# Linear attention in 32x32 tiles over four pairs, with turns in blocks of 32 on VectorE

## The chip, the cores and the metric

The kernel runs on one core of a Trainium2 chip. The metric is the time of one execution on the device in microseconds (us), from the first to the last instruction of the core; lower is better. A profile is one such execution, taken by the hardware profiler. Engines are called PE (TensorE), PEld (its weight loads), DVE (VectorE), ACT (ScalarE), POOL (GpSimd) and SP (the engine that issues the DMAs).

## The reference

The input x has 16 images of 256 channels and 64 x 64 pixels, in fp32. There are two layers, each with a group normalization ahead of it and the input added behind it. The first is a grouped 3x3 convolution whose weights are rotated per image, times a factor per channel. The second is linear attention with 8 heads of 32 channels, and a depthwise 5x5 sum of the values:

```
q, k, v = xt @ Wq.T + bq, ...           # xt: tokens x channels of the normalized image
q = (relu(q) + 1e-06) / scale           # k likewise
q = q**3 / norm(q**3) * norm(q)         # k likewise
z = 1 / (q . k.sum(tokens) + 1e-06)     # per token and head
out = (q @ (k.T @ v)) * z + depthwise5x5(v)
out = out @ Wproj.T + bproj
```

## The kernel before

Images are worked through one after the other; parts of image b + 1 (its convolution) and of image b + 2 (statistics of its input) are put between the steps of image b. The order is written out by hand: each engine does its instructions in the order of the source, so that an instruction that waits holds up all behind it on its engine. All DMAs are issued by SP, in order too. The tokens of an image are taken in 32 tiles of 128; two of them make a pair m, and an image has NP = 16 pairs.

*Key steps* (`key_step`, L718; 16 per image, of which the first three are done inside the attention of the image before). `key_products` multiplies two tiles by the key and value weights (L525, 128x512), `key_bias` adds the bias and applies relu on DVE, `squares` (ACT), `cube` (POOL, L504), `ratio` (DVE) and `root` (POOL, L513) make the factor norm / norm, `key_scale` (ACT) applies it, `values` (L558) sums k.T @ v and the keys' sum over the tokens in two PSUM banks. `key_store` writes the values to DRAM (vpad), from which `load_blocks` reads them back as vh for the depthwise sum.

*Between* (`between`, L741): the first query products, the first of the four convolutions of the next image (`convolve`, L358: 9 taps, each in 16 tiles of 32x32 at once, into four banks), the last values, the depthwise sum of the first half (`depthwise`, L593, 8 x 16 products into fm by ACT).

*Attention steps* (`attention_step`, L779; one per pair, with the steps of neighbouring pairs one behind the other). `blocked` (L610, ACT) copies a pair's pixels into blocks of 8 x 4, `query_products` (L618) and `query_bias` make q with the tokens on the partitions; `squares`, `cube`, `ratio`, `root` give its factor. `turn` (L634, PE) and `turned` (L639, ACT) put the channels on the partitions. `attend` (L642) multiplies by the masked state kvx (L651), so that the result has the tokens on the partitions and 33 columns per head, the last of which is the denominator: z has 16 numbers per partition (two tiles, 8 heads; L653, L656), the product with z (L660, DVE) and the sum with fm (L662, POOL) follow. `turn_back` (L670, PE; L672, ACT) turns it, `project` (L680) multiplies by Wproj, `add_up` (L692, DVE) adds bias and input, and `store` writes two pairs at a time. Convolutions 1 to 3 of the next image are begun in steps 3, 7 and 11 (UNITS) and moved out in the step behind (`evict`, L371, ACT; `settle`, L381 and L382, DVE); the rows for each are loaded into one buffer, xr, by `load_rows`. The second half of the depthwise sum is in step 9 (SECOND). fm, xr and vh have one buffer each. Five PSUM banks go round (`bank`), two hold the sums of values and then pn (kv0, kv1), one the small products.

`more_stats` (L700) takes the statistics of a part of image b + 2 on DVE (L107) and issues the load of the next part, which goes into the same buffer. `prepare` (L184) makes the rotated weights of image b + 2.

Of the kernel before, what the change touches and what calls it, by code (L numbers as in the profile page):

```python
# [9 lines left out]
F32 = mybir.dt.float32  # L10
# [5 lines left out]
P = 128  # L16
C = 256
# [11 lines left out]


UNITS, SECOND = {3: 1, 7: 2, 11: 3}, 9

STATS = {3: (0, 1), 5: (2,), 7: (3, 4), 9: (5, 6), 11: (7,)}
# [6 lines left out]
NV = 6  # L40
# [6 lines left out]
K_ID, K_G8, K_GM, K_CG, K_SG, K_SEL, K_END = 0, 128, 256, 260, 278, 296, 424  # L47
# [3 lines left out]
def conv_attention(ctx: ExitStack, tc: tile.TileContext, x, consts, kw, b1, w2, b2, b2r,  # L51
# [11 lines left out]
    rp = pool("rows", 2)  # L63
    op = pool("outs", 2)
# [4 lines left out]
    ps = pool("ps", 5, space=PSUM)  # L69
    psk = pool("psk", 1, space=PSUM)  # L70
    pss = pool("pss", 1, space=PSUM)
# [43 lines left out]
    ident = ct[:, K_ID:K_ID + P]  # L115
# [11 lines left out]
    phalf = const("phalf", [P, 2])  # L127
    nc.gpsimd.memset(phalf, 0.5)
    pi2 = const("pi2", [P, 1])
# [21 lines left out]
    def gn_coefs(st, b, which):  # L151
# [6 lines left out]
        mean, var = mv[:, :, 0], mv[:, :, 1]  # L158
        co = sp.tile([P, 5, 2], F32, tag=f"co{which}", name=f"co{which}_{b}")
        a, pooled, d, v, m = (co[:, k, :] for k in range(5))  # L160
        pm = pss.tile([P, 2], F32, tag="small", name=f"pm{which}_{b}")
# [6 lines left out]
        pv = pss.tile([P, 2], F32, tag="small", name=f"pv{which}_{b}")  # L168
# [5 lines left out]
        if which == 0:  # L174
            nc.vector.tensor_mul(pooled, d, a)
        return a, pooled, m
# [7 lines left out]
    def prepare(b):  # L184
# [9 lines left out]
        ph = pss.tile([HID, 2], F32, tag="small", name=f"ph_{b}")  # L194
# [8 lines left out]
        pa = pss.tile([P, 2 + 2 * HD], F32, tag="small", name=f"pa_{b}")  # L203
# [21 lines left out]
        pe = pss.tile([P, NH], F32, tag="small", name=f"pedge_{b}")  # L225
# [63 lines left out]
        def shifts(t):  # L289


            pb = pss.tile([P, 3], F32, tag="small", name=f"pbias_{b}_{t}")
# [6 lines left out]
            nc.vector.tensor_scalar(shift[:, t, 3:4], shift[:, t, 3:4], -1.0, None, ALU.mult)  # L299
# [66 lines left out]
    def evict(b, u, q):  # L366

        i, t = 2 * u + q // 2, q % 2
        if t == 0:
            state[b]["x"][i] = xp.tile([P, 2, CH], F32, tag="x", name=f"x_{b}_{i}")  # L370
        nc.scalar.activation(state[b]["x"][i][:, t, :], state[b]["pc"][q], AF.Identity,  # L371
                             bias=state[b]["shift"][:, t, 3:4])

    def settle(b, u, q):
# [5 lines left out]
        e = xt[:, t, :].rearrange("p (r w) -> p r w", w=W)[:, :, 0:W:W - 1]  # L380
        nc.vector.tensor_add(e, e, shift[:, t, 0:3:2].unsqueeze(1).to_broadcast([P, ROWS, 2]))  # L381
        nc.vector.bn_stats(state[b]["st1"][:, t, i, :], xt[:, t, :])  # L382

    load_kernels(0)
    for _ in prepare(0):
        pass
# [5 lines left out]
    wp_t = const("wp", [P, 2, C], halves(wp))  # L392
    bp_t = const("bp", [P, 2], bp)
    dwb_t = const("dwb", [P, 2], dwb)
# [34 lines left out]
    for (w, br), lo in zip(wl.values(), (0, 2 * C)):  # L429
        for t in range(2):  # L430
            nc.vector.tensor_mul(w[:, t, 0:C], w[:, t, 0:C], inv_t)
        nc.vector.tensor_mul(br[:, 0:C], br[:, 0:C], inv_t[0:1])
        n = w.shape[2]
        nc.sync.dma_start(wscr[:, :, lo:lo + n], w)
        nc.sync.dma_start(bscr[:, lo:lo + n], br)

    pb = pss.tile([P, 2], F32, tag="small", name="pb")
    for co in range(2):
        for t in range(2):
            nc.tensor.matmul(pb[:, co:co + 1], lhsT=wp_t[:, t, ts(co, P)], rhs=dwb_t[:, t:t + 1],  # L440
                             start=t == 0, stop=t == 1)
    nc.vector.tensor_add(bp_t, bp_t, pb)
# [47 lines left out]
    def focus(r, name):  # L490
        return {"r": r, "name": name, "s": sp.tile([P, 4, 2], F32, tag="s", name=f"s_{name}", bufs=5)}

    def relu(f):
        nc.vector.scalar_tensor_tensor(f["r"], f["r"], 0.0, eps_t.unsqueeze(1).to_broadcast([P, 2, C]),  # L494
                                       ALU.max, ALU.add)
# [10 lines left out]
    def ratio(f, inverse):  # L506
        s2, s6, q = (f["s"][:, k, :] for k in range(3))
        over, under = (s6, s2) if inverse else (s2, s6)
        nc.vector.reciprocal(q, under)
        nc.vector.tensor_mul(q, q, over)  # L510
# [479 lines left out]
```

## Time and profile before

| what | value |
| --- | --- |
| time, median of 3 runs | 3762.31 us (3759.23 to 3769.41) |
| the profiled execution: time / span | 3763.77 us / 3762.0 us |
| granted PE clock, mean | 0.988 |
| busy: PE / PEld / DVE / ACT / POOL | 95% / 74% / 65% / 54% / 44% |
| DMA | 513.78 MB, 137 GB/s, share of 16 engines 44.3% |

A row of the groups names line, engine, operation, what is written and read, shapes and count; behind the bar stand the busy time in us and the mean of one instruction in ns; behind the second bar the idle time of the engine ahead of it and what ended it. A row of the timeline has the start in us, the length of the merged piece, and the same names. A row of stages has the stretch, its length, the busy time of PE, PEld, DVE, ACT and POOL with their instructions, the granted clock, the share of the DMA engines and their GB/s. Ends of PE's instructions are modelled and reach into the next one; starts are exact. Each fp32 product is two records on PE, each fp32 turn one. DVE's idle time is no cost as long as another engine sets the end.

### The profile page before, as it was taken

Reading aid. Unit: us, or ns where it says so; the run is one execution under the profiler, and the core shown is the slowest. Engines: PE = TensorE matmul, PEld = TensorE weight load, DVE = VectorE, ACT = ScalarE, POOL = GpSimd, SP = SyncE. Lnnn points to the kernel's source line nnn. Section 1 sums busy time; section 2 is a strip of 40 time slices with the busy share of each in tenths; the row PEclk is TensorE's granted clock in tenths of the full one; section 3 lists DMA queues with packets and bytes.
Section 4 is the critical chain, followed back from the end, with each engine's and each line's share of the span. In section 5 each row is a group of like instructions: output and inputs, shape, how many; then the busy total and the mean of one; then the engine's idle time right before and its main releaser. Section 6 shows DMA issues by size and latency. Waiting matters only on the chain. (4 is left out here: it accounts for less than half of the span.)

```text
span 3762.0 us, 102026 instructions
## 1 busy us (share of the span) xinstructions
PE 3568.1 (95%) x40424; PEld 2769.5 (74%) x40424; DVE 2435.6 (65%) x6403; ACT 2013.1 (54%) x6501; POOL 1638.3 (44%) x1775
## 2 busy tenths in 40 slices
PE   5899999999999999999999999999999999999999
PEld 3577777777777777687777777777777777777778
DVE  5756667566675656667666675666856667566656
ACT  2455645556455555654646455464555645555555
POOL 3343535344353444534445353343534535344445
PEclk9999999999999999999999999999999999999999
DMA  6453544525445254452634535355353544524332
GB/s 175 130 155 95 156 145 128 171 83 159 144 143 164 81 169 126 145 169 87 175 114 148 169 100 175 94 153 156 110 175 95 155 145 145 163 77 151 103 131 105
DMA packets 219807, 513.78 MB, mean 137 GB/s; under 512 B 26645, under 2 KB 99863, under 8 KB 207044
## 3 DMA queue, kind: packets, MB, share of 16 engines
q1 hardware_dynamic: 219332, 507.26, 44.3%
q8 instruction: 320, 5.24, 0.6%
q14 instruction: 155, 1.27, 0.1%
HBM read 371.63 MB, written 135.53 MB: 135 GB/s over the span
## 5 line engine op out<-in xcount | busy, mean ns | idle before, releaser
L525 PE MATMUL pk<-wkv,x 128*128 128x512 f32 x2048 | 989.4, 624 | 0.0
L662 POOL TENSOR_TENSOR o<-o,fm 128x256 f32<-128x256 f32 x512 | 362.9, 730 | 1045.0 <-DVE o L660 890.1
L525 PEld LDWEIGHTS pk<-wkv,x 128*128 128x128 f32 x2048 | 611.4, 312 | 191.3 <-issue 16.1
L358 PE MATMUL pc<-xr,wt 32*32 32x504 f32 (+1 forms) x17856 | 616.9, 596 | 8.2 <-issue 4.2
L358 PEld LDWEIGHTS pc<-xr,wt 32*32 32x32 f32 x17856 | 360.7, 103 | 227.2 <-issue 88.3
L680 PE MATMUL py<-oT,wp 128*128 128x256 f32 x2048 | 507.2, 390 | 11.8 <-ACT oT L672 11.7
L618 PE MATMUL pq<-wq,xq 128*128 128x256 f32 x2048 | 492.0, 383 | 22.4 <-ACT qT L639 20.4
L501 ACT ACTIVATE r_k<-rk 128x256 f32<-128x256 f32 x1024 | 415.4, 407 | 177.2 <-DVE rk L494 109.7
L371 ACT ACTIVATE x<-pc,shift 128x512 f32<-128x512 f32 x256 | 165.4, 690 | 527.7 <-PE pc L358 527.7
L501 ACT ACTIVATE r_q<-rq 128x256 f32<-128x256 f32 x1024 | 413.9, 408 | 59.0 <-POOL rq L504 32.3
L618 PEld LDWEIGHTS pq<-wq,xq 128*128 128x128 f32 x2048 | 370.0, 191 | 84.8 <-ACT qT L639 27.1
L680 PEld LDWEIGHTS py<-oT,wp 128*128 128x128 f32 x2048 | 368.0, 189 | 60.5 <-ACT oT L672 15.8
L672 ACT COPY oT<-po 128x512 f32<-128x512 f32 x256 | 150.0, 586 | 455.4 <-PE po L670 454.9
L626 DVE TENSOR_TENSOR rq<-pq,bq 128x512 f32<-128x512 f32 x256 | 176.1, 688 | 335.5 <-PE pq L618 328.2
L513 POOL TENSOR_TENSOR s_k<-s_k,phalf 128x2 f32<-128x2 f32 x256 | 177.0, 692 | 483.8 <-DVE s_k L510 472.7
L547 ACT ACTIVATE rk<-rk,s_k 128x256 f32<-128x256 f32 x512 | 231.8, 500 | 243.5 <-POOL s_k L513 243.5
L533 DVE TENSOR_TENSOR rk<-pk,bkv 128x256 f32<-128x256 f32 x512 | 214.7, 419 | 225.5 <-PE pk L525 222.6
L504 POOL TENSOR_TENSOR rk<-r_k,rk 128x512 f32<-128x512 f32 x256 | 326.8, 1277 | 66.2 <-ACT r_k L501 65.4
L558 PEld LDWEIGHTS pkv<-v,rk 128*128 128x128 f32 x2048 | 271.1, 194 | 111.2 <-issue 51.8
L504 POOL TENSOR_TENSOR rq<-r_q,rq 128x512 f32<-128x512 f32 x256 | 329.7, 1288 | 29.9 <-issue 29.9
L513 POOL TENSOR_TENSOR s_q<-s_q,phalf 128x2 f32<-128x2 f32 x256 | 179.4, 701 | 368.2 <-DVE s_q L510 366.8
L558 PE MATMUL pkv<-v,rk 128*128 128x132 f32 x2048 | 275.1, 281 | 21.5 <-ACT rk L547 21.5
(128 smaller groups left out, 5369.9 us busy)
## 6 DMA issues: line engine op xcount, KB each, us to landing
vh<-vpad SPq DMA_DIRECT2D x256, 384.0 KB
vh<-vpad SPq DMA_DIRECT2D x256, 360.0 KB
vpad<-v SPq DMA_DIRECT2D x512, 128.0 KB
out<-x SPq DMA_DIRECT2D x128, 512.0 KB
xr<-in_x SPq DMA_DIRECT2D x186, 320.0 KB
xs<-in_x SPq DMA_DIRECT2D x224, 256.0 KB
xr<-in_x SPq DMA_DIRECT2D x62, 288.0 KB
xs<-in_x SPq DMA_DIRECT2D x16, 512.0 KB
```

The lines of the kernel that those rows point to most:

```text
L358: nc.tensor.matmul(pcs[q].rearrange("p (r w) -> p r w", w=W)[ts(j, HD), :, to:to + n], lhsT=wt[ts(q, HD), j, k, :], rhs=g[ts(q, HD), j, r: ...
L501: nc.scalar.activation(f["r2"][:, j, :], f["r"][:, j, :], AF.Square, accum_out=f["s"][:, k, j:j + 1])
L504: nc.gpsimd.tensor_mul(f["r"], f["r2"], f["r"])
L513: nc.gpsimd.tensor_tensor(f["s"][:, 3, :], f["s"][:, 2, :], phalf, ALU.pow)
L525: nc.tensor.matmul(pm, lhsT=state[b]["x"][n // 2][:, t, T % BC:CH:BC], rhs=w[:, t, :], start=t == 0, stop=t == 1)
L533: nc.vector.tensor_add(f["r"][:, j, :], pm[:, 0:C], br[:, 0:C])
L547: nc.scalar.mul(f["r"][:, j, :], f["r"][:, j, :], f["s"][:, 3, j:j + 1])
L558: nc.tensor.matmul(pkv[hh], lhsT=r[:, j, ts(hh, P)], rhs=vbuf[n % NV][:, j, :, 4 * hh:4 * hh + 4], start=T == 0, stop=T == NT - 1,)
L618: nc.tensor.matmul(pq[:, j, :], lhsT=xq[:, t, ts(j, P)], rhs=w[:, t, :], start=t == 0, stop=t == 1)
L626: nc.vector.tensor_add(f["r"], f["pq"], state[b]["q"][1].unsqueeze(1).to_broadcast([P, 2, C]))
L662: nc.gpsimd.tensor_add(o, o, fm[:, 2 * (m % NCH) + j, :])
L680: nc.tensor.matmul(py[:, co].rearrange("p y (J c) -> p J y c", c=BC), lhsT=wp_t[:, t, ts(co, P)], rhs=oT[:, t, :].rearrange("p (J y c) -> ...
```

## The change

Attention now goes over a group g of PG = 4 pairs at once, four groups per image, and keeps the channels on the partitions behind it.

- `evict` writes the convolved image in the order of blocks (8 x 4 pixels), so that `blocked` is gone and the queries read it directly; it adds the projection's bias as well (in shift). The two edge columns are corrected by POOL, once for both halves of the channels, instead of by DVE. The statistics take the bias out and put it back (`gn_coefs`).
- The queries are scaled on ACT (`scale`), and `ratio` and `root` are done for two pairs of queries at once. The 1e-06 of relu is in the bias; relu is one tensor_tensor with max.
- `query_turn`: DVE turns the queries in blocks of 32x32 (one instruction of 128x512 per pair, 16 per image) instead of PE and ACT.
- `spread_state`: one product spreads the state over four row groups; kvd holds, per half a and head d of four, a 32x32 block of the state (k = 0) and the keys' sum repeated over 32 columns (k = 1).
- `attend(b, g, a)`: 32 products of 32x32 tiles with 256 columns, 16 tiles at once, into four banks: per partition 256 numerators and 256 denominators, one per channel. There are 8 of them per image.
- `divide`: ACT copies the denominators out and adds 1e-06, DVE takes the reciprocal of 128x512 and multiplies it with the numerators, twice per half group. `join` adds it on POOL to fm in place.
- `depthwise` gives fm by head and channel; `turn_blocks` turns it in blocks on DVE, in place (two instructions of 128x1024 per group).
- `project` multiplies 512 columns at a time, straight from fm; `turn`, `turned` and `turn_back` are gone. `add_up` adds x and writes into fm, and the store goes out from there.
- Six banks go round, and all the small products and pn take theirs among them. The scratch tiles of rows (tag r1) have four buffers. The values have five buffers instead of six.
- The order of the steps is new (`between`, `group`, `lead`). Query pairs 0 to 3 are made in `between`; group g makes the queries of group g + 1. Convolutions 1, 2 and 3 stand in groups 0, 1 and at the head of group 2, the second half of the depthwise sum behind convolution 3, the three early key steps of the next image in group 3. The rows of the next convolution are loaded at the end of groups 0 and 1.
- The setup computes the projection's bias ahead of the first kernels.

The diff, cut (of functions that are rewritten, the new lines; the old ones stand above):

```diff
-    ps = pool("ps", 5, space=PSUM)
+    ps = pool("ps", 6, space=PSUM)
     psk = pool("psk", 1, space=PSUM)
-    pss = pool("pss", 1, space=PSUM)
...
-        nc.scalar.activation(state[b]["x"][i][:, t, :], state[b]["pc"][q], AF.Identity,
+        xt = state[b]["x"][i][:, t, :].rearrange("p (J y c) -> p y J c", y=BR, c=BC)
+        nc.scalar.activation(xt, state[b]["pc"][q].rearrange("p (y J c) -> p y J c", y=BR, c=BC), AF.Identity,
                              bias=state[b]["shift"][:, t, 3:4])
     def settle(b, u, q):
         if u == 0 and q == 0:
             state[b]["st1"] = sp.tile([P, 2, NCH, 6], F32, tag="st1", name=f"st1_{b}")
         xt, shift = state[b]["x"][i], state[b]["shift"]
-        e = xt[:, t, :].rearrange("p (r w) -> p r w", w=W)[:, :, 0:W:W - 1]
-        nc.vector.tensor_add(e, e, shift[:, t, 0:3:2].unsqueeze(1).to_broadcast([P, ROWS, 2]))
+        if t == 0:
+            e = xt[:, 0, 0:1]
+            e = bass.AP(e.tensor, e.offset, [e.ap[0], [CH, 2], [BC, BR], [CH - BR * BC + BC - 1, 2]])
+            nc.gpsimd.tensor_add(e, e, shift[:, :, 0:3:2].unsqueeze(2).to_broadcast([P, 2, BR, 2]))
...
-        nc.vector.scalar_tensor_tensor(f["r"], f["r"], 0.0, eps_t.unsqueeze(1).to_broadcast([P, 2, C]),
-                                       ALU.max, ALU.add)
+        nc.vector.tensor_tensor(f["r"], f["r"], eps_t.unsqueeze(1).to_broadcast([P, 2, C]), ALU.max)
...
+    def ratio(s):
+        nc.vector.reciprocal(s[:, 2], s[:, 1])
+        nc.vector.tensor_mul(s[:, 2], s[:, 2], s[:, 0])
+    def root(s):
+        nc.gpsimd.tensor_tensor(s[:, 3], s[:, 2], phalf[:, 0:s.shape[2]], ALU.pow)
+    def scale(f):
+        for j in range(2):
+            nc.scalar.mul(f["r"][:, j, :], f["r"][:, j, :], f["s"][:, 3, j:j + 1])
...
+    def spread_state(b):
+        pr = bank(f"pr_{b}")[:, 0:2 * (HD + 1) * 4]
+        nc.tensor.matmul(pr, lhsT=sel, rhs=state[b]["kvx"].rearrange("p a c h -> p (a c h)"), start=True, stop=True)
+        pr = pr.rearrange("p (a c h) -> p a h c", a=2, h=4)
+        kvd = qp.tile([P, 2, 2, 4, HD], F32, tag="kvd", name=f"kvd_{b}")
+        nc.scalar.copy(kvd[:, 0], pr[:, :, :, 0:HD])
+        nc.vector.tensor_copy(kvd[:, 1], pr[:, :, :, HD:HD + 1].to_broadcast([P, 2, 4, HD]))
+        state[b]["kvd"] = kvd
...
+            state[b]["fm"] = fmp.tile([P, 2, NT * 2, HD], F32, tag="fm", name=f"fm_{b}_{half}")
+        fm = state[b]["fm"].rearrange("p a B c -> p c (a B)")
+        vb = vh.rearrange("p R J (c a d) -> p c d a (R J)", a=2, d=4)
         pd = bank(f"pd_{b}_{half}_{c}").rearrange("p (k n) -> p k n", k=4)
         for k in range(4):
...
+            for d in range(4):
                 nc.tensor.matmul(
...
+                    pd[ts(d, HD), k, :].rearrange("p (a B) -> p a B", a=2),
                     lhsT=band_t[:, c + k, :],
...
+                    rhs=vb[:, c + k, d],
                     start=True, stop=True,
...
+                    tile_position=(0, HD * d),
                 )
...
+        nc.scalar.copy(fm[:, c:c + 4, :], pd)
+    def turn_blocks(b, g):
+        for a in range(2):
+            v = state[b]["fm"][:, a, ts(g % 2, NT), :].rearrange("p B c -> p (B c)")
+            nc.vector.transpose(v, v)
...
+                nc.tensor.matmul(pq[:, j, :], lhsT=state[b]["x"][i][:, t, ts(2 * R + j, P)], rhs=w[:, t, :],
                                  start=t == 0, stop=t == 1)
...
+    def query_turn(b, m):
+        if m % PG == 0:
+            state[b]["qT"] = qp.tile([P, PG, 2 * C], F32, tag="qT", name=f"qT_{b}_{m}")
+        nc.vector.transpose(state[b]["qT"][:, m % PG, :], state[b]["f"].pop(m)["r"].rearrange("p j n -> p (j n)"))
+    def attend(b, g, a):
+        qT = state[b]["qT"].rearrange("p m (j h n) -> p (m j) h n", j=2, h=NH)
+        pns = [bank(f"pn_{b}_{g}_{a}_{q}") for q in range(4)]
+        for k in range(2):
+            for d in range(4):
+                for q in range(4):
+                    nc.tensor.matmul(
+                        pns[q][ts(d, HD), ts(k, C)].rearrange("p (B n) -> p B n", n=HD),
+                        lhsT=state[b]["kvd"][ts(q, HD), k, a, d, :],
+                        rhs=qT[ts(q, HD), :, 4 * a + d, :],
+                        start=True, stop=True,
+                        tile_position=(HD * q, HD * d),
+                    )
+        state[b]["pn"] = pns
+    def divide(b, g, a):
+        state[b]["o"] = []
+        for c in range(2):
+            o = rp.tile([P, 2, C], F32, tag="r1", name=f"o_{b}_{g}_{a}_{c}")
+            for k in range(2):
+                pn = state[b]["pn"][2 * c + k]
+                nc.scalar.activation(o[:, k, :], pn[:, C:2 * C], AF.Identity, bias=eps1)
+            nc.vector.reciprocal(o, o)
+            for k in range(2):
+                nc.vector.tensor_mul(o[:, k, :], state[b]["pn"][2 * c + k][:, 0:C], o[:, k, :])
+            state[b]["o"].append(o)
+    def join(b, g, a):
+        fm = state[b]["fm"][:, a, ts(g % 2, NT), :].rearrange("p (B q) n -> p q B n", q=4)
+        for c, o in enumerate(state[b]["o"]):
+            v = fm[:, ts(c, 2)]
+            nc.gpsimd.tensor_add(v, v, o.rearrange("p k (B n) -> p k B n", n=HD))
+    def project(b, i):
+        fm = state[b]["fm"].rearrange("p a B n -> p a (B n)")
+        state[b]["py"] = []
+        for co in range(2):
+            py = bank(f"py_{b}_{i}_{co}")
             for t in range(2):
...
+                nc.tensor.matmul(py, lhsT=wp_t[:, t, ts(co, P)], rhs=fm[:, t, ts(i % 4, CH)],
...
+            state[b]["py"].append(py)
+    def add_up(b, i):
+        xt = state[b]["x"].pop(i)
+        y = state[b]["fm"].rearrange("p a B n -> p a (B n)")[:, :, ts(i % 4, CH)]
         for co in range(2):
...
+            nc.vector.tensor_add(*(v.rearrange(o, y=BR, c=BC) for v, o in (
+                (y[:, co, :], "p (y J c) -> p J y c"), (state[b]["py"][co], "p (J y c) -> p J y c"),
+                (xt[:, co, :], "p (J y c) -> p J y c"))))
+        nc.sync.dma_start(halves(out[b])[:, :, ts(i, CH)], y)
...
+        chain = iter(())
+        if g == 2:
+            if more:
+                convolve(b + 1, 3)
             for c in range(0, HD, 4):
                 depthwise(b, 1, c)
+                if more and 4 <= c <= 16:
+                    evict(b + 1, 3, c // 4 - 1)
+            turn_blocks(b, 2)
+            if more:
+                for q in range(4):
+                    settle(b + 1, 3, q)
+                chain = norm1(b + 1)
+                next(chain)
             if b + 2 < B:
...
+                more_stats(b + 2, 6)
+        if g < 3:
+            A = PG * (g + 1)
+            attend(b, g, 0)
+            divide(b, g, 0)
+            join(b, g, 0)
+            query(b, A)
+            squares(f[A], 0)
+            cube(f[A])
+            query(b, A + 1)
+            attend(b, g, 1)
+            if g == 2:
+                next(chain, None)
+                if b + 2 < B:
+                    more_stats(b + 2, 7)
+                if more:
+                    fold_load(b + 1, "kv")
+            squares(f[A + 1], 0)
+            cube(f[A + 1])
+            divide(b, g, 1)
+            squares(f[A], 1)
+            join(b, g, 1)
+            query(b, A + 2)
+            squares(f[A + 1], 1)
+            ratio(f[A]["s2"])
+            root(f[A]["s2"])
+            squares(f[A + 2], 0)
+            cube(f[A + 2])
+            if g == 2:
+                next(chain, None)
+            query(b, A + 3)
+            scale(f[A])
+            scale(f[A + 1])
+            squares(f[A + 3], 0)
+            cube(f[A + 3])
+            query_turn(b, A)
+            query_turn(b, A + 1)
+            if g < 2:
+                if more:
+                    convolve(b + 1, g + 1)
+                if g == 1 and b + 2 < B:
+                    more_stats(b + 2, 3)
+                for n in range(8):
+                    load_blocks(b, 16 + 8 * g + n)
+            squares(f[A + 2], 1)
+            squares(f[A + 3], 1)
+            ratio(f[A + 2]["s2"])
+            root(f[A + 2]["s2"])
+            if g == 2:
+                next(chain, None)
+            scale(f[A + 2])
+            scale(f[A + 3])
+            query_turn(b, A + 2)
+            query_turn(b, A + 3)
+            if g != 1:
+                turn_blocks(b, g + 1)
+            if g == 1 and b + 2 < B:
+                more_stats(b + 2, 4)
+        else:
+            if more:
+                lead(b + 1, 0)
+                next(made, None)
+            attend(b, g, 0)
+            divide(b, g, 0)
+            join(b, g, 0)
+            if more:
+                lead(b + 1, 1)
+                next(made, None)
+            attend(b, g, 1)
+            divide(b, g, 1)
+            join(b, g, 1)
+            if more:
+                lead(b + 1, 2)
+                next(made, None)
+        for c in range(2):
+            project(b, 2 * g + c)
+            if more and g < 2:
+                for q in (2 * c, 2 * c + 1):
+                    evict(b + 1, g + 1, q)
+                for q in (2 * c, 2 * c + 1):
+                    settle(b + 1, g + 1, q)
+            if g == 2 and c == 0:
+                next(chain, None)
+            add_up(b, 2 * g + c)
+        if g < 2:
+            if g == 1 and b + 2 < B:
+                more_stats(b + 2, 5)
+            if more:
+                load_rows(b + 1, g + 2)
```

## What the change was predicted to do

> **What bounds the kernel now.** I read part 1 of the page first, then the stages of one image in the middle of the run, then the order of time on PE in the attention stage.
>
> ```profile
> PE 3568.1 (95%) x40424; PEld 2769.5 (74%) x40424; DVE 2435.6 (65%) x6403; ACT 2013.1 (54%) x6501; POOL 1638.3 (44%) x1775
> ```
> ```profile
> 1518.40:1586.90 68.50, 64.48 (x293) 47.76 (x292) 53.00 (x137) 44.74 (x154) 40.50 (x37) 0.98 0.55 173
> 1586.90:1610.20 23.30, 23.30 (x587) 18.47 (x585) 8.22 (x22) 13.67 (x40) 5.86 (x6) 1.00 0.39 88
> 1610.20:1747.00 136.80, 132.25 (x1648) 105.45 (x1647) 90.74 (x241) 65.98 (x210) 55.18 (x67) 1.00 0.43 131
> ```
> The rows are the key steps, the stage between, and attention (columns: length, then busy PE, PEld, DVE, ACT, POOL, clock, DMA share, GB/s). PE fills every stage; DVE has 152.0 of 228.6 us. The first value product of an image starts at 1522.10 and the next one's at 1751.76, so an image takes 229.7 us. The first query product of image 0 is near 209, the last image's at 3652, and 109 us follow it: 209 + 15 x 229.6 + 109 = 3762, the profiled execution's span (its time is 3763.8, the median 3762.3; the sums below are against the span).
>
> ```profile
> 1639.06 1.07 PE L651 MATMUL pn<-kvx,qT 128*128 128x132 f32 x8
> 1639.96 1.99 PE L680 MATMUL py<-oT,wp 128*128 128x256 f32 x8
> 1641.79 0.60 PE L634 MATMUL pt<-consts,rq 128*128 128x128 f32 x4
> 1642.22 1.89 PE L618 MATMUL pq<-wq,xq 128*128 128x256 f32 x8
> 1643.95 0.60 PE L670 MATMUL po<-consts,o 128*128 128x128 f32 x4
> ...
> 1657.86 9.71 PE L358 MATMUL pc<-xr,wt 32*32 32x512 f32 x288
> ```
> Starts count, since ends overlap. A pair costs PE 0.90 (pn), 1.82 (py), 0.44 + 0.44 (turns), 1.73 (pq); each starts as the last one ends. A four-byte product is two records.
>
> **Part by part, PE.** Per image 64 + 64 transposes go: 128 x 0.148 (0.59 for 4) = 19.0 us. Projection keeps its columns in twice as long products: 64 records at 0.444 (pk: 8 in 3.55) = 28.4 for 16 x 1.82 = 29.1. The 16 x 0.90 = 14.4 of pn become 8 x 64 records of 32x32 tiles. Bounds: the convolution's 33.3 ns a record (9.6 us / 288) gives 17; half of that, as columns are half as many, 8.5. The depthwise sum's 27.9 (7.13 / 256) gives 1.8 us a half group, 14.3 in all; I take it. The state's spreading adds 0.3. PE falls from 220 to 200.6 us.
>
> **ACT and POOL.** ACT loses xq, oT, qT (480.7 us, 30.0 an image) and gains 32 query scalings at 0.45 and 32 denominators at 0.40: 123 for 126. POOL joins 16 x 1.28 for 22.7, does 8 fewer roots, gains 8 edge sums at 0.1 to 0.7: about 100 for 102. Neither total binds; their latencies do. The setup's projection bias moves ahead of the first kernels: at most 3 us, once.
>
> **DVE** carries the change.
> ```profile
> L656 DVE RECIPROCAL zz<-zz 128x16 f32<-128x16 f32 x256 | 64.8, 253 | 8.8
> ...
> L420 DVE RECIPROCAL soft<-soft 128x256 f32<-128x256 f32 x1 | 1.8, 1752 | 0.0
> ```
> The denominators were 16 numbers per partition and pair; now they are spread over the 32 channels, and a reciprocal has 512. The rows give (1752 - 253) / 240 = 6.25 ns an element, so 3.35 us for 512; 16 of them 53.6 us. [...] The block transposes have no row. Nearest is one-source work on 512 elements in SBUF (bn_stats, L382, 0.69): 16 query turns at 0.69 = 11.0, and 8 block turns of 1024 at 1.22 (0.42 for 256 and 0.69 for 512 continued) = 9.8. [...] the dear end is two passes for four bytes, 20.8 more. Away go L653 and L656, L381 (to POOL), half of the query ratios (L509, L510): 15.6; add_up goes from 13.9 to 11.0. The new relu still reads two SBUF tensors (L494's median 0.69, mean 0.85 when POOL is busy): zero. DVE: 152 + 53.6 + 20.8 + 0.4 - 18.5 = 208 us an image, more than PE's 200.6.
>
> **The waits.** Sums don't set the end: the new order makes them alternate. A division (one reciprocal and two products, twice) is 2 x (3.35 + 0.82) = 8.35. Count group 0 from T, the end of its first division. The second half of attend writes four of the six banks, and the first half's four come free only at T: PE has done its two queries (3.5) and stands. DVE does two biases with relu (2.8), ACT squares the second (0.8) and only then, in its order, copies two denominators (0.9): the reciprocal starts at T + 4.5, the division ends at T + 12.85. The convolution needs those banks too, so PE stands again and runs to T + 22.5. DVE: biases, relus, ratio to T + 16; first pair of turns to T + 17.8; then it waits for square (17.9), cube on POOL (1.28), square (0.8), ratio (0.4), root (0.7), scale (0.85 each): last turn at 23.5, block turns 25.9, settle and add_up, each twice (1.3 each), 31.2. The next attend waits for the first add_up's bank and both projections (T + 29.3): next division from T + 32.0 to T + 40.3. A group with convolution lasted 1657.86 - 1624.95 = 32.9.
>
> Entry to group 2 is the worst place. The last rows (xr, one buffer) are loaded in SP's order behind two stores that wait for add_up, and a statistics load that waits for DVE (T + 32.5). Four issues take 1.6 and 1.25 MB at some 220 GB/s 6 us, more behind 1.5 MB: T + 42. Queued behind the convolution (9.6) on PE is the depthwise sum (7.2), behind that ACT's last copy (0.6), and behind that on DVE the block turns (2.4), settle, aggregate and statistics (4.5), then the division: T + 75. DVE has nothing for 27 us of it. The rest of group 2 (29.8 to its last add_up by the same steps) and group 3 with the three early key steps (DVE 2 x 8.35 + 3 x 2.3, projections and add_up, two bank waits) are 62. Stage between: PE 26.7, the last scale and turn 2.1, settle, block turns and statistics 5, division 8.35: 42.2. Key steps keep 68.4, since 13 x (3.55 + 0.90) stay.
>
> Sum: 68.4 + 42.2 + 40.3 + 75 + 62 = 288 us an image.
>
> PE's standing has a price of its own.
> ```profile
> 1572.95 0.59 PE L295 MATMUL pbias<-gm,rsum 128*32 128x1 f32 x24 [2.77 <-DVE rsum L279]
> ```
> ```profile
> 1574.00:1577.40 3.40, 3.40 (x8) 1.75 (x8) 2.18 (x11) 3.33 (x11) 1.64 (x2) 0.52 0.97 352
> ```
> One wait of 2.8 us is followed by 3.4 us at a clock of 0.52. [...] Waits of 5 to 12 us come some ten times an image[...], each losing 1.7 us of PE; where DVE's chain is later (half of them) nothing shows. I add 10: 298. The last image has no convolution and no early keys: 33 + 38 + 48 + 62 + 5 = 186. Total 209 + 15 x 298 + 186 = 4865.
>
> **Rivals.** (a) Not slower: the rest of DVE's 208 us beside its 53 in the key steps is 155; if it ran without a wait, an image took 68.4 + 155 = 224, and the kernel 209 + 15 x 224 + 151 = 3720 (the last image's 186 less some 35 of its waits). It decides where DVE's waits outside the key steps stay below 6 us an image. For it: PE has 20 us fewer and could run ahead. Against: six banks, four taken by each half, and waits of 7 in each group and 27 in one. 6% (1% of it within 0.3% of no change, about what a measurement here can tell). (b) The hole ahead of group 2 closes, because the rows arrive early or the copies overlap: 298 - 29 = 269, 4427. Against: SP's order. 13%. (c) Turns of four-byte blocks take two passes; all of the 20.8 lies on the path: 319, about 5190. 15%. Mine has 62%; 4% are worse still (POOL and DVE hindering each other in the chain).
>
> **Numbers.** 4865 is the likeliest. Range 4350 to 5250: my case with its unknowns (attend 8.5 to 17, clock 0 to 20), most of (b) and (c). Faster 0.05, same 0.01, slower 0.94.
>
> **What would show it.** PE and DVE near 70% each; a reciprocal row 128x512 of 3.35 us, 256 times; block transposes of 0.69 and 1.22; pn waiting for DVE's o; the DVE block turns waiting for ACT's fm, some 27 us, once an image; pc waiting for the xr load; granted clock below 0.95. I'm wrong if the reciprocal is far under 3 us, or if PE stays above 85% busy.

## The result and the profile after

The changed kernel takes 5410.78 us (median of 4 runs, 5408.72 to 5412.74) where the kernel before takes 3765.57 on the same chip (4 runs, 3759.23 to 3769.41): 1.4371 times as long, 95% interval 1.4347 to 1.4396. The prediction was 4865, with a range of 4350 to 5250: the direction is right, and so are most of the waits that it names, but one cost is missing from its sum and the size is wrong. 546 us are missing, or 34 us of each image. The profiled execution took 5411.7 us, its span is 5409.9, its mean granted clock 0.858.

Part 1 of the page after, to be read against the same line of before:

```profile
PE 4236.3 (78%) x43528; PEld 2692.4 (50%) x43528; DVE 3437.1 (64%) x5557; ACT 2170.9 (40%) x6517; POOL 1634.7 (30%) x1519
```

No engine is above 80% any more, as foreseen. But PE's busy time has grown by 668 us, where the prediction took 16 x 19.4 = 310 away. The groups show which lines swelled (busy us, mean ns | idle ahead of it and what ended it):

```profile
L674 DVE RECIPROCAL o<-o 128x512 f32<-128x512 f32 x256 | 855.3, 3341 | 80.7 <-ACT o L673 80.3
...
L607 PE MATMUL pd<-vh,band 107*32 107x128 f32 x8192 | 609.1, 456 | 0.2 <-DVE fm L702 0.2
...
L620 DVE STREAM_TRANSPOSE fm<-fm 128x1024 f32<-128x1024 f32 x128 | 150.1, 1211 | 639.3 <-ACT fm L614 639.3
```
```profile
L702 DVE TENSOR_TENSOR fm<-py,x 128x512 f32<-128x512 f32 x256 | 168.4, 692 | 290.2 <-DMA out<-fm 253.9 <-PE py L693 11.3 <-POOL co L171 10.2
```

The reciprocal and the turns cost what was forecast. The depthwise sum (pd) does not: in the kernel before the same 8192 records had a mean of 273 ns.

```profile
L593 PE MATMUL pd<-vh,band 107*32 107x128 f32 x8192 | 234.6, 273 | 2.6 <-issue 2.5
```

The convolutions and the queries are busy longer too (616.9 and 492.0 us before), although their products have the same shapes. What of it is work at half clock and what is rows that still land comes up below.

```profile
L359 PE MATMUL pc<-xr,wt 32*32 32x504 f32 (+1 forms) x17856 | 805.4, 680 | 384.8 <-DMA xr<-in_x 246.3 <-issue 137.2 <-ACT x L374 1.3
L628 PE MATMUL pq<-wq,x 128*128 128x256 f32 x2048 | 585.8, 447 | 40.9 <-DVE o L676 30.8 <-DVE fm L702 10.1
```

And `add_up` (L702) waits 253.9 us for the store of fm, a wait that the prediction does not have. Here is one image of after in stages, cut at the points from which the prediction counts: from the first query product to the end of the first division (T), group 0, group 1 to the first division of group 2, the rest, the key steps (columns as before).

```profile
2217.42:2272.54 55.12, 47.40 (x688) 35.03 (x687) 32.59 (x43) 28.54 (x69) 12.76 (x12) 0.95 0.32 93
2272.54:2315.57 43.03, 33.72 (x464) 19.81 (x465) 32.98 (x39) 15.67 (x52) 12.86 (x12) 0.86 0.30 92
2315.57:2413.70 98.13, 69.37 (x1008) 40.84 (x1009) 40.82 (x53) 27.41 (x64) 14.16 (x16) 0.80 0.26 78
2413.70:2482.88 69.18, 50.02 (x273) 26.59 (x274) 54.91 (x79) 19.80 (x74) 21.43 (x18) 0.73 0.15 49
2482.88:2549.67 66.79, 62.53 (x292) 46.85 (x291) 55.24 (x136) 42.76 (x144) 39.73 (x36) 1.00 0.58 175
```

Predicted were 42.2, 40.3, 75, 62 and 68.4, together 288 and 298 with the clock's 10. Measured: 332.25. Two stages carry most of the miss, 12.9 and 23.1 us, and they are the two that hold a half of the depthwise sum. PE's order of time shows it at the entry to group 2:

```profile
2341.35 7.13 PE L693 MATMUL py<-fm,wp 128*128 128x512 f32 x16
2364.10 15.77 PE L359 MATMUL pc<-xr,wt 32*32 32x512 f32 x288 [15.62 <-DMA xr<-in_x]
2379.79 18.34 PE L607 MATMUL pd<-vh,band 107*32 107x128 f32 x256
```

The convolution starts 48.5 us after the third stage begins (forecast: 42) and lasts 15.8 us (9.6); the depthwise half behind it lasts 18.3 us (7.2). The three differences, 6.5 + 6.1 + 11.1 = 23.7, are that stage's miss of 23.1, but for 0.6. In the first stage the other half lasts 12.55 + 7.29 us (2236.91 and 2250.04), 12.6 more than forecast. Of the rest, group 0 misses 2.7 and the rest of groups 2 and 3 7.2; the key steps are 1.6 shorter than forecast.

### The profile page after: what moved, and what is told of

Its sections match the earlier page's. It is cut to its first block, busy times and chain, and to the rows that moved or that the text cites. A ratio compares the mean times of both kernels' runs of the same rounds, so it can differ in the third digit from the quotient of the medians.

```text
span 5409.9 us, 106863 instructions
## 1 busy us (share of the span) xinstructions
PE 4236.3 (78%) x43528; PEld 2692.4 (50%) x43528; DVE 3437.1 (64%) x5557; ACT 2170.9 (40%) x6517; POOL 1634.7 (30%) x1519
## 5 line engine op out<-in xcount | busy, mean ns | idle before, releaser
L359 PE MATMUL pc<-xr,wt 32*32 32x504 f32 (+1 forms) x17856 | 805.4, 680 | 384.8 <-DMA xr<-in_x 246.3
L674 DVE RECIPROCAL o<-o 128x512 f32<-128x512 f32 x256 | 855.3, 3341 | 80.7 <-ACT o L673 80.3
L684 POOL TENSOR_TENSOR fm<-fm,o 128x512 f32<-128x512 f32 x256 | 323.0, 1262 | 1673.0 <-DVE o L676 1370.6
L658 PE MATMUL pn<-qT,kvd 32*32 32x256 f32 x8192 | 360.1, 528 | 385.5 <-DVE o L676 326.5
L628 PE MATMUL pq<-wq,x 128*128 128x256 f32 x2048 | 585.8, 447 | 40.9 <-DVE o L676 30.8
L693 PE MATMUL py<-fm,wp 128*128 128x512 f32 x1024 | 530.4, 668 | 107.3 <-DVE sk L514 64.3
L607 PE MATMUL pd<-vh,band 107*32 107x128 f32 x8192 | 609.1, 456 | 0.2 <-DVE fm L702 0.2
L614 ACT COPY fm<-pd 128x512 f32<-128x512 f32 x256 | 306.5, 1206 | 742.2 <-PE pd L607 728.0
L620 DVE STREAM_TRANSPOSE fm<-fm 128x1024 f32<-128x1024 f32 x128 | 150.1, 1211 | 639.3 <-ACT fm L614 639.3
L628 PEld LDWEIGHTS pq<-wq,x 128*128 128x128 f32 x2048 | 452.1, 228 | 168.0 <-issue 45.3
L607 PEld LDWEIGHTS pd<-vh,band 107*32 107x32 f32 x8192 | 428.6, 128 | 177.2 <-issue 30.9
L521 ACT ACTIVATE rk<-rk,sk 128x256 f32<-128x256 f32 x512 | 231.9, 500 | 459.0 <-POOL sk L517 459.0
L702 DVE TENSOR_TENSOR fm<-py,x 128x512 f32<-128x512 f32 x256 | 168.4, 692 | 290.2 <-DMA out<-fm 253.9
```

What stands on the lines that cost most here:

```text
L359: nc.tensor.matmul(pcs[q].rearrange("p (r w) -> p r w", w=W)[ts(j, HD), :, to:to + n], lhsT=wt[ts(q, HD), j, k, :], rhs=g[ts(q, HD), j, r: ...
L521: nc.scalar.mul(f["r"][:, j, :], f["r"][:, j, :], f["s"][:, 3, j:j + 1])
L607: nc.tensor.matmul(pd[ts(d, HD), k, :].rearrange("p (a B) -> p a B", a=2), lhsT=band_t[:, c + k, :], rhs=vb[:, c + k, d], start=True, stop ...
L614: nc.scalar.copy(fm[:, c:c + 4, :], pd)
L628: nc.tensor.matmul(pq[:, j, :], lhsT=state[b]["x"][i][:, t, ts(2 * R + j, P)], rhs=w[:, t, :], start=t == 0, stop=t == 1)
L658: nc.tensor.matmul(pns[q][ts(d, HD), ts(k, C)].rearrange("p (B n) -> p B n", n=HD), lhsT=state[b]["kvd"][ts(q, HD), k, a, d, :], rhs=qT[ts ...
```

## Experiments

The theory after this reading: (1) the read pattern of the depthwise sum, single elements 1 KB apart in place of runs of eight, makes it 2.5 times as long; (2) the entry to group 2 is late because rows and stores stand in each other's way; (3) PE's clock falls while it waits; the reciprocals lie on the path, as predicted. The rivals are stated with each run. The medians of before on the same chip were 3763 to 3770 in all of them; each ratio is to the median measured with that run.

### The read pattern

**Pairs of heads side by side** (e1). The values are stored so that two heads are neighbours, and the depthwise sum reads runs of two; it computes the same. The edit, cut:

```diff
...
-        vb = vh.rearrange("p R J (c a d) -> p c d a (R J)", a=2, d=4)
+        vb = vh.rearrange("p R J (c d a) -> p c d (R J) a", a=2, d=4)
...
-                    pd[ts(d, HD), k, :].rearrange("p (a B) -> p a B", a=2),
+                    pd[ts(d, HD), k, :].rearrange("p (B a) -> p B a", a=2),
...
```

> The changed kernel, with the values stored in an order in which the two heads of a depthwise product lie side by side (8 bytes read together instead of 4, still 1 KB from pair to pair). Theory: the depthwise records take 71.6 ns instead of 27.9[...];[...] they come down to 28 to 31 ns, a half image's sum from 18.3 to 7.5 us, and with both halves on the path 22 us an image: about 5060 us. Rival 1: every separate place costs, however many elements lie there: about 50 ns, half the gain, 5240. Rival 2: the records are slow because PE's clock is down and ACT's copies hold the banks: no change of the records, 5400.

Measured: 5172.66 us, 1.3733 of before (1.3693 to 1.3773), 238 us less than the changed kernel.

```profile
L607 PE MATMUL pd<-vh,band 107*32 107x128 f32 x8192 | 312.5, 313 | 4.9 <-DVE fm L702 3.9 <-ACT fm L614 1.0
```

From 609 us to 312, not to 235: two elements to a run bring back most of the rate. A half image takes 9.72 us from its start to that of the next product, for 7.14 in the kernel before (here first this run, then the kernel before):

```profile
2275.08 9.79 PE L607 MATMUL pd<-vh,band 107*32 107x128 f32 x256
2284.80 2.04 PE L658 MATMUL pn<-qT,kvd 32*32 32x256 f32 x64
```
```profile
1676.99 7.20 PE L593 MATMUL pd<-vh,band 107*32 107x128 f32 x256
1684.13 0.66 PE L670 MATMUL po<-consts,o 128*128 128x128 f32 x4
```

What the remaining 10 ns a record are is open, since in this form the products are also written alternately, 64 columns apart.

**The new read in the kernel before** (e6). Clock and neighbours are those of before, only the depthwise read is new; its values come out in wrong places.

```diff
-        vb = vh.rearrange("p R (m j) (c h) -> p R m j c h", j=4, h=NH)
+        vb = vh.rearrange("p R J (c a d) -> p c d a (R J)", a=2, d=4)
...
-                    rhs=vb[:, :, :, j, c + k, :],
+                    rhs=vb[:, c + k, j],
```

> The kernel before, with nothing of the change but the pattern in which its depthwise sum reads the moving operand (single elements 1 KB apart, as the changed kernel reads them, instead of runs of eight heads); the depthwise values come out in wrong places, so that the output isn't the reference's. Theory: the read pattern alone makes a half-image of the depthwise sum 18.3 us instead of 7.3, whatever the clock and the other changes; before is bound by PE, so 32 x 11.0 = 353 us come on top of 3766: 4080 to 4140 us, mean of the depthwise record near 450 ns instead of 273. Rival (the changed kernel's lower clock, its other PSUM banks or its loads slow these matmuls, not the pattern): within 1% of 3766, mean near 273 ns.

Measured: 4101.19 us, 1.0897 (1.0875 to 1.0919), at a clock of 0.988.

```profile
L593 PE MATMUL pd<-vh,band 107*32 107x128 f32 x8192 | 577.8, 449 | 0.0
```
```profile
1732.09 18.32 PE L593 MATMUL pd<-vh,band 107*32 107x128 f32 x256
```

The same 18.3 us for a half image as in the changed kernel: it is the pattern and nothing around it. PE's 343 us more appear almost whole in the time (336), because before is bound by PE (95% busy).

**The old read in the changed kernel** (e10), the same edit the other way round (values in wrong places again).

> The changed kernel with the depthwise sum reading as the kernel before reads it, in runs of eight heads (the values then stand in wrong places, so the output isn't the reference's; everything else is as it was). Theory: the rate of the matmuls is set by the length of the runs alone, mean back to 273 ns, 374 us less of PE's time; 80% of what the pairs saved on PE came off the time (238 of 297), so 5110 us (5060 to 5130). Rival (the lower clock of the changed kernel or its banks have a part in it): mean over 290 ns and above 5140 us.

Measured: 5156.44 us, 1.3687 (1.3658 to 1.3716).

```profile
L607 PE MATMUL pd<-vh,band 107*32 107x128 f32 x8192 | 241.3, 275 | 10.7 <-ACT fm L614 6.0 <-DVE fm L702 4.7
```

The mean is back at 275 ns, so the cause of the longer depthwise sum is settled; but of 368 us that PE is relieved of only 254 come off the time, 69% where the estimate said 80. A part of the gain is caught by the next wait. The row of attend's products, here first, then in the changed kernel:

```profile
L658 PE MATMUL pn<-qT,kvd 32*32 32x256 f32 x8192 | 382.8, 536 | 447.7 <-DVE o L676 327.7 <-DVE qT L647 101.6 <-DVE fm L702 13.7
```
```profile
L658 PE MATMUL pn<-qT,kvd 32*32 32x256 f32 x8192 | 360.1, 528 | 385.5 <-DVE o L676 326.5 <-DVE qT L647 47.1 <-DVE fm L702 11.7
```

With the first depthwise half done earlier, PE stands before the first attend of an image until DVE has turned the queries: that wait goes from 47.1 to 101.6 us.

### The entry to group 2

**The store in two halves of the channels** (e2).

```diff
-        nc.sync.dma_start(halves(out[b])[:, :, ts(i, CH)], y)
+        for co in range(2):
+            nc.sync.dma_start(out[b, ts(co, P), ts(i, CH)], y[:, co, :])
```

> The changed kernel, with each store split in its two halves of the channels. The whole store spans rows that lie interleaved with those of the next add_up, and the order of the instructions shows that add_up waits for it; the halves don't touch, and that wait isn't in the program any more. Theory: the 254 us that DVE waited for stores (7.9 us ahead of group 2, 1.8 in groups 0 and 1, more in groups 2 and 3) lay on the path, and the rows of the last convolution come 8 us sooner: 10 to 16 us an image, 5150 to 5260 us. Rival: the rows come no sooner, because the DMA engines are what they wait for: less than 5 us an image, above 5330.

Measured: 5317.43 us, 1.4118 (1.4077 to 1.4159): 93 us less, between the two. The wait for the store is gone from `add_up`, and a part of it comes back as a wait for PE:

```profile
L702 DVE TENSOR_TENSOR fm<-py,x 128x512 f32<-128x512 f32 x256 | 169.5, 684 | 76.0 <-PE py L693 74.8 <-POOL co L171 0.8
```

So it was a wait of the store's shape, not of the data: two stores of the same bytes don't hold up the next write (presumably since the extent of one store over both halves covers what `add_up` writes next; that wasn't looked into); most of the convolution's wait for its rows remains:

```profile
L359 PE MATMUL pc<-xr,wt 32*32 32x504 f32 (+1 forms) x17856 | 808.5, 685 | 318.9 <-DMA xr<-in_x 182.1 <-issue 136.2 <-ACT x L374 0.7
```

**The rows ahead of the stores** (e3): `load_rows(b + 1, 3)` is issued ahead of group 1's projections.

```diff
+            if g == 1 and more:
+                load_rows(b + 1, 3)
...
-            if more:
-                load_rows(b + 1, g + 2)
+            if more and g == 0:
+                load_rows(b + 1, 2)
```

> The changed kernel, with the load of the last convolution's rows ahead of the stores of its group in SP's order. Theory: the convolution at the head of group 2 waits 15.6 us for rows that were issued 17 us after the buffer was free; issued there, they land about 10 us sooner, and the convolution starts warmer: 10 to 15 us an image, 5190 to 5260 us. Rival: the depthwise sum and the copies behind it would wait for something else (the values' blocks, the store of fm): under 4 us an image, above 5350.

Measured: 5329.82 us, 1.415 (1.4109 to 1.4192): 81 us less. DVE's hole shrank by 218 us, from 639.3 to 421.7, and `add_up`'s wait for the store grew by 134:

```profile
L620 DVE STREAM_TRANSPOSE fm<-fm 128x1024 f32<-128x1024 f32 x128 | 150.1, 1211 | 421.7 <-ACT fm L614 421.7
```
```profile
L702 DVE TENSOR_TENSOR fm<-py,x 128x512 f32<-128x512 f32 x256 | 168.0, 689 | 428.6 <-DMA out<-fm 387.8 <-PE py L693 17.0 <-issue 9.1
```

The gain is what the one wait lost less what the other took: 84, near the measured 81. The new order moves part of the wait from the rows to the stores; that the two share the DMA engines is the likely reason, and wasn't tested.

**A busy PE ahead of the convolution** (e8, e9, e11). Matmuls of 128x128 without use are put into an idle bank before the fourth convolution; three runs differ in their number.

```diff
+        if u == 3 and b:
+            fill = psk.tile([P, P], F32, tag="kv0", name=f"fill_{b}")
+            for _ in range(110):
+                nc.tensor.matmul(fill, lhsT=wp_t[:, 0, 0:P], rhs=wp_t[:, 0, 0:P], start=True, stop=True)
```

With 110:

> The changed kernel with 110 matmuls of 128x128 without use, into a bank that is idle then, put ahead of the fourth convolution of every image, where PE waits some 15 us for its rows. Theory: the convolution takes 15.8 us behind the wait because PE's clock was taken down in it, and 9.6 us with a busy PE ahead; it is on the path: 15 x 6 = 90 us less, 5310 to 5330 us, and the wait for the rows falls to 2 us or less in that place. Rival 1 (the clock falls for another reason, the mean load): the convolution stays at 15 us, 5400 to 5420. Rival 2 (the fill outlasts the wait): over 5430.

Measured: 5450.2 us, 1.448 (1.4459 to 1.4502), rival 2.

```profile
2351.62 24.73 PE L355 MATMUL fill<-wp 128*128 128x128 f32 x220
2376.28 9.67 PE L363 MATMUL pc<-xr,wt 32*32 32x512 f32 x288
```

The fill was sized too long, but the convolution behind it is short: 9.67 us. With 64:

> The fill ahead of the fourth convolution once more, shorter: the 110 matmuls ran 24.7 us (0.225 us each) and outlasted the wait of 15.6 by some 9 us, so 64 of them, 14.4 us. Theory: the convolution, which took 15.8 us behind the idle wait and 9.67 us behind the long fill, takes 9.7 again and starts when it did: 15 x 6.1 = 92 us less than 5411, 5310 to 5335 us. Rival: what follows the convolution waits for a transfer or for VectorE anyway, and the 6 us reappear there: 5390 to 5420.

Measured: 5426.56 us, 1.4407 (1.4372 to 1.4442): no gain, and for another reason than the rival's. Stages of PE alone behind the fill (length, busy PE with its records, clock, DMA share, GB/s):

```profile
2364.30:2367.60 3.30, 0.00 (x0) 1.00 1.02 209
2367.60:2371.00 3.40, 2.92 (x5) 0.69 0.61 125
2371.00:2375.50 4.50, 4.50 (x82) 0.50 0.01 4
2375.50:2382.80 7.30, 7.30 (x219) 0.99 0.02 4
```

The convolution "starts" when the first of its four row loads lands, does 5 records in 3.4 us while the others land (these count as busy), then runs 4.5 us at half clock and the rest at full (a record that lies in two stages is counted in both). The unmodified changed kernel has the same picture at 2364.10:

```profile
2363.00:2366.00 3.00, 1.90 (x3) 0.50 1.01 204
2366.00:2368.30 2.30, 2.30 (x4) 0.50 0.22 46
2368.30:2372.70 4.40, 4.40 (x82) 0.50 0.02 4
2372.70:2379.80 7.10, 7.10 (x219) 1.00 0.02 5
```

So its 15.8 us are, by this estimate, 9.67 of work, some 2.2 of clock and some 3.9 of rows that are not there yet. With 84:

> The fill ahead of the fourth convolution with 84 matmuls (18.9 us). Behind the fill of 64 PE was idle for 3.4 us, ran two products a microsecond for 2 us more while the last of the four row loads landed, and then stood at half clock for 4.4 us: the fill had bought nothing. Reading of that: of the 6.1 us that the convolution is longer than 9.67, some 3.9 are rows that still land and 2.2 are the clock. Theory: a fill that ends as the last rows land leaves the convolution at 9.7 us and full clock, and saves the clock's part only: 15 x 2.2 = 33 us less than the 5427 of the fill of 64, 5385 to 5400 us. Rival (the clock is all of the 6.1 us): 5330 to 5345. Rival 2 (the clock's part is hidden behind VectorE): 5415 to 5440.

Measured: 5407.99 us, 1.4363 (1.4338 to 1.4389): 19 us less than the fill of 64 and 3 us less than no fill, which is within the interval.

```profile
2334.90:2353.70 18.80, 18.80 (x169) 1.00 0.70 202
2353.70:2365.40 11.70, 11.42 (x289) 1.00 0.04 10
```

Full clock throughout, and the convolution ends 30.5 us after the projection ends; without a fill it ended 31.5 us after (2348.3 to 2379.8), with 64 33.0. SP gets to the last row load later in both runs with a fill: it is done with issuing it 13.1 us behind the projection's end with 64 and 12.4 with 84, for 11.6 without; why is open. From that moment to the convolution's end it is 20.0 us with 64, 18.2 with 84 and 19.9 without. So some 30 us of this stretch are the rows' way and the work itself, and the clock's part is about 1.7. Theory (3) explains little of this stretch: the clock does fall there, but a fill that held it gained nothing that can be measured. That the clock costs as little in the other places wasn't tried.

### The reciprocals, and all together

**No reciprocal** (e4): the line is taken out; numerators are multiplied by the denominators, so this is no division.

```diff
-            nc.vector.reciprocal(o, o)
```

> The changed kernel without the reciprocals of 512 (the numerators are multiplied by the denominators; the result of attention is another one). Theory: every division lies on the path, 8 x 2 x 3.34 = 53.5 us an image: 855 us less, 4555. Rival: PE's own work and DVE's other waits fill part of it: half, about 4980.

Measured: 4550.35 us, 1.2081 (1.2045 to 1.2117). The 855.3 us of the group come off whole (860): in sum the reciprocals lay on the path. The run doesn't tell whether each of them did, since the granted clock rose as well, from 0.858 to 0.918. Attend's row tells how they did: PE waited for the division's banks.

```profile
L658 PE MATMUL pn<-qT,kvd 32*32 32x256 f32 x8192 | 250.9, 440 | 104.1 <-DVE qT L647 47.9 <-DVE o L675 41.4 <-DVE fm L701 14.6
```

The convolutions of groups 0 and 1 need those banks too. In the changed kernel they start, in two pieces, just behind the products that free the banks (DVE at 2281.17 and 2285.29):

```profile
2281.70 1.34 PE L359 MATMUL pc<-xr,wt 32*32 32x512 f32 x4 [1.91 <-issue]
2285.81 12.00 PE L359 MATMUL pc<-xr,wt 32*32 32x512 f32 x284 [2.77 <-issue]
```

Their idle time "issue" falls from 137.2 to 12.0 us without the reciprocals:

```profile
L359 PE MATMUL pc<-xr,wt 32*32 32x504 f32 (+1 forms) x17856 | 727.2, 623 | 275.4 <-DMA xr<-in_x 260.5 <-issue 12.0 <-DVE sq L514 1.4
```

**Pairs, two stores and early rows together** (e5), which still computes what the reference does:

> The changed kernel with the three repairs together: two heads side by side in the depthwise read, the store in two halves, and the rows of the fourth convolution loaded ahead of group 1's stores. Theory: the causes are separate, the savings add up: 238 + 93 + 81 = 412, so about 5000 us (4970 to 5030). Rival: the last two take away the same wait (one queue of transfers, late rows), so the larger of them counts once: 5170 - 93 = 5080 (5050 to 5110).

Measured: 5071.39 us, 1.3474 (1.3451 to 1.3496). The rival holds: beside the pairs the two moves bring 101, not 174. They take away one wait: the convolutions wait for rows 182.1 us with the two stores (246.3 without), 183.1 with the early rows, and beside the pairs 187.0 with both (256.1 with neither).

**The same without reciprocals** (e7; no division, as in e4):

> The same three repairs and no reciprocal (the numerators are multiplied by the denominators, so the division isn't one). Theory: the reciprocals' 860 us come off in full beside the repairs, 4110 to 4170 us: still slower than before, so that the path of the attention, turn by turn between PE and VectorE, costs over 300 us even without the division and with the pattern mended. Rival: with the reciprocals gone, PE or the transfers bound the image and hide part of the 860: 4250 to 4400 us.

Measured: 4158.22 us, 1.1049 (1.1027 to 1.1071). Even without its division and with the three repairs the new attention is 393 us slower than before. Here the reciprocals were worth 913 us, more than their busy time. No run points to a form that beats the kernel before.

**Old read, two stores, early rows** (e12; depthwise values in wrong places):

> The changed kernel with the depthwise sum reading in runs of eight heads (values in wrong places, the output isn't the reference's) together with the store in two halves and the early rows. Theory: beside the pairs these two moves were worth 101 us (5173 to 5071), here as much: 5156 - 101 = 5055 us (5035 to 5075); with all that the prediction left out mended, its sum of 4865 is still missed by 190, by its waits and the clock. Rival: with the depthwise sum short, the rows and stores are what comes last, and the moves are worth their full 93 + 81: 4980 us (4965 to 5000).

Measured: 5041.29 us, 1.3388 (1.3358 to 1.3419), near the first. It leaves 176 us to the predicted 4865. One of its images takes 310.7 us (first convolution at 2079.20 and 2389.89). Its entry to group 2 still reads

```profile
2209.79 16.19 PE L359 MATMUL pc<-xr,wt 32*32 32x512 f32 x288 [13.04 <-DMA xr<-in_x]
```

so the rows are late in every form that was tried.

## Why the prediction missed, point by point

**The step that failed: the depthwise sum at its old price.** The prediction's stages count "the depthwise sum (7.2)" in group 2 and as much within "PE 26.7" in the stage between, and its list of what PE loses and gains has no entry for it. The diff shows the change: `vb[:, :, :, j, c + k, :]` became `vb[:, c + k, d]`, whose innermost step is a block of 256 channels. It was put at its old price, and no reason was given. Measured: 19.8 and 18.3 us in place of 7.2 twice, 23.8 us an image on PE. Undoing it alone (e10) gives back 254 us of the 546, or 15.9 an image, the rest of it going into the wait for the queries' turns and other waits; the 5156 us that are left would have lain within the stated range.

This case gives the new form's price: 27.9 ns from record to record (7.14 / 256) for runs of eight, 38.0 (9.72 / 256) for pairs, 71.4 (18.28 / 256, from 2379.79 to attend's start at 2398.07) for single elements. With pairs the rate of runs of eight was not reached. Whether a run of two can reach it is not shown here, since the way of writing changed too.

**The transfers at the entry to group 2.** The place was right ("the worst place") and so was the resource, "T + 42" was 48.5. The sum had the rows behind the stores, but no wait of `add_up` for its own store (253.9 us), and it let the convolution start with all rows there: it started on the first of four loads. The two moves are worth 101 us beside the pairs and 115 beside the old read, 6 to 7 us an image. This step was under-sized as well, but its place and kind were forecast.

**The clock.** 10 us an image were added for it, the author's estimate from one stretch of the kernel before (3.4 us at 0.52); the granted mean is 0.858. In the one place where it was tested, keeping the clock up gained 3 us over the whole run. Elsewhere the traces give a bound. Taken in steps of half a microsecond, PE is busy at half clock for about 61 us of the image shown, so that about 31 us of its busy time would fall away at full clock: 2 in the first stage, 5 in group 0, 11 and 13 in the two stages behind it, none in the key steps; in an image of the kernel before it is 2. This is an estimate, and too high as a cost, since rows that still land count as busy and DVE's chain hides some of it. In group 0 it is on the path: the convolution ends 25.2 us behind T for a forecast of 22.5, which is the stage's whole miss of 2.7, and its main piece takes 12.0 us, of which the first 4.9 are at half clock.

The prediction's reading of its row, that a short gap is paid for, doesn't hold each time. The gap of that row, 2.8 us ahead of the product of L295 (L296 in the changed kernel), comes back in most images. In the kernel before, the clock was down in the 4.5 us behind it in 13 of 14 cases (means of 0.50 to 0.70), in the changed kernel in 8 of 14 (0.50 to 0.62): its mean from 2202.30 on is 0.50, and from 2537.40 on, an image later, 1.00.

**What remains.** 176 us (11 us an image) are not separated. Where they stand is seen in e12: from the first division of group 1 to that of group 2 it has 86 us (2164.96 to 2251.01) for the predicted 75, of which 6.6 are the longer convolution and 2.8 its later start; the stage between, group 0 and the rest are 3 to 5 over each, the key steps nothing. Together that is 22.7 us over 288, of which 10 were allowed for the clock. The same estimate of the clock's part is 32 us in that image, so the clock alone could fill the gap; that it does is not shown.

**What held.** The reciprocal: 3341 ns for a forecast of 3.35 us, 256 times, and leaving it out is worth its 855 us (860 in e4, 913 in e7). The turns: 0.72 and 1.21 us for 0.69 and 1.22, so rival (c) is out. DVE's work: 216.5 us in the image shown, for 208. DVE's block turns wait for ACT's fm once an image, 40 us on average (639.3 / 16) and not 27; with pairs it is 33 (525.2 / 16, e1), so the depthwise sum is 7 or more of the 13, and the convolution in the same hole is longer too. Attend's price of 1.8 us holds only where it runs in one piece at full clock (1.49 at a clock of 1.00 from 2398.07 on, 2.34 at 0.52 from 2259.94 on): over the run it is busy 360.1 us, 22.5 an image for 14.3, as half of them stand in two pieces around a wait for banks and some run at half clock. Group 0, built step by step: 43.0 for 40.3. Rival (a) is refuted in its condition, DVE's waits outside the key steps below 6 us: they are 265.5 - 161.3 = 104 us in the image shown. Rival (b), the hole that closes, has its test in e3: a third of the hole closed and the time fell by 81 us only, and the wait for stores grew.

**Why a change that takes work from PE is slower.** Before, PE was busy 95% of the time, whatever the other engines did. After, two halves of each group alternate between PE and DVE over six banks, and the 53.5 us of reciprocals an image, 512 numbers per partition for 16, are added end to end. With the old read pattern it is still 37% slower (e10), without the reciprocals 21% (e4), and with the three repairs and no reciprocals 10% (e7).

## What to carry to other kernels

An index pattern that a diff turns round is a cost item like any other (here 71.4 ns a record for 27.9): write down the innermost run of each operand, before and after, and if it falls to one element, look for a row with such runs or bound it from above. A sum over stages has to contain each instruction of the stage at its new form, also those that the change is not about. And before a wait is called the clock's or a transfer's, look at the first microseconds behind it record by record: a long "busy" piece may be an engine that is being fed by loads that still land (here 6 records in the first 4.2 us of a piece of 15.8, from 2364.10 on).

## What the hardware showed that was not expected

- Matmuls of fp32 with 128 columns, four column groups of 32 at a time: 27.9, 38.0 and 71.4 ns a record for runs of eight, two and one element in the moving operand (7.14, 9.72 and 18.28 us for 256 records); the kernel before gives the last one too when it reads in that way (18.10, e6, 1565.51 to 1583.61).
- An idle stretch of 3.4 us on PE, with a busy PE ahead of it, was followed by half clock from 1.3 us behind its end on, for 6.8 us (e9, 2368.9 to 2375.7). A gap of 2.8 us, always ahead of the same product, was followed in the changed kernel by a mean clock of 0.50 to 0.62 over 4.5 us in 8 images and of 1.00 in 6.
- The label "issue" ahead of a product stood for a wait for PSUM banks: 137.2 us of it went down to 12.0 when the division that frees them became shorter.
